# A perceiver megakernel: the second linear attention's query features get their 0.1 from ScalarE

## The chip, the cores and the metric

The kernel runs on one core of a Trainium2 chip. Its time is the device time of one execution in microseconds. Three runs were made; the figure used is their median. A separate execution was recorded by the hardware profiler, and all rows below come from it. The core has five engines with queues of their own: TensorE (PE in the rows, with PEld for its weight loads), VectorE (DVE), ScalarE (ACT), GpSimd (POOL) and SyncE (SP), which issues most transfers.

## The reference, cut to what matters

The program is a chain of eleven residual blocks over 16 sequences of 64 tokens, 256 wide (1024 tokens in all): three layers of cross attention, self attention and a feed-forward block, and a last layer that ends with its attention. The change lies in the eighth block, the self attention of the third layer, which the reference writes as

```python
def _spherical_features(x, projection):
    x_norm = x / (jnp.linalg.norm(x, axis=-1, keepdims=True) + 1e-08)
    proj = jnp.einsum('bhsd,hfd->bhsf', x_norm, projection)
    return jax.nn.relu(proj) + YAT_EPS          # YAT_EPS = 0.1
...
Qp = _spherical_features(Q, projection)
Kp = _spherical_features(K, projection)
KV = jnp.einsum('bhsf,bhsd->bhfd', Kp, V)
QKV = jnp.einsum('bhsf,bhfd->bhsd', Qp, KV)
K_sum = jnp.sum(Kp, axis=2)
normalizer = jnp.einsum('bhsf,bhf->bhs', Qp, K_sum)[..., None]
out = QKV / jnp.maximum(normalizer, 1e-06)
```

It has 16 heads of 16 channels, and 64 features for each head. Q, K and V are linear maps of the normalized input; the result goes through one more linear map and is added to the input. The query features `Qp` are the rectified projection plus 0.1.

## The kernel before

The eleven blocks are methods that issue their instructions one after the other; a tile framework places buffers, derives the waits from the data, and may order instructions within the engines' queues. Inside `l2_attn` (lines 1947 to 2118) `self.pinned` is on, so TensorE's instructions (issued by `mm`, line 2619, and `tr`, line 2631) keep the order in which the program writes them. `awake` issues matmuls whose result nobody reads.

`linear(i)` prepares one half of the tokens (512 of 1024) and is a generator, so that its steps can be laid between other work: it normalizes and transposes the input, and ScalarE copies the transposed blocks to `xT` (line 1989); `lin` multiplies by the weights for q, k and v; VectorE adds the biases (`z`, line 2007, and `va`, line 2003); ScalarE squares, VectorE sums and inverts the norms, GpSimd scales (`z`, line 2019); the scaled q and k are transposed to `qn` and `nT` (copies of line 127 on VectorE and 129 on ScalarE). Then come the query features: for each of two groups of channels, TensorE makes `pqp` in a PSUM tile of four banks (`quad`, one buffer, shared with the keys' `pkp`), ScalarE rectifies it into `qp` in SBUF (line 2040), and GpSimd adds 0.1 to the 128x2048 numbers in place (line 2041). So these two lines run twice in each half, four times in all.

The loop at line 2103 goes over eight blocks of 128 tokens and two steps more. Step t makes the keys' features of block t (`pkp` on TensorE, then `kp` on VectorE, line 2055, with maximum and 0.1 in one instruction), multiplies the queries of block t-1 with the sums of their sequences (`acc`, in `apply`, which reads `qp`), runs some steps of `linear(1)` while t is below 4, forms the sums of block t (`pk`, then four masked products `kv` on VectorE, lines 2070 and 2071), and projects block t-2 (`lin` with `wo`), adds it to `x` (line 425) and takes its mean and variance (`measured`, lines 145 and 146). For every second block `factors` turns the variance into a factor: a small multiply-add on VectorE (line 153), a root on ScalarE (line 154) and a reciprocal on VectorE (line 155). The query features of the second half come in step 3; they are read from step 5 on. Those of the first half come before step 0 and are read from step 1 on.

Of the kernel before, what the change touches and what calls it, by code (L numbers as in the profile page):

```python
# [12 lines left out]
F32 = mybir.dt.float32  # L13
I32 = mybir.dt.int32
BF16 = mybir.dt.bfloat16
AF = mybir.ActivationFunctionType
ALU = mybir.AluOpType
# [3 lines left out]
P = 128  # L21
# [43 lines left out]
class Sections:  # L65
# [1881 lines left out]
    def l2_attn(self):  # L1947
        nc, tc, d = self.nc, self.tc, self.d
        F, HT = 64, NT // 2
        with ExitStack() as ctx:  # L1950
            sb = ctx.enter_context(tc.tile_pool(name="l2a", bufs=1, side="right", reuse_waits="tile"))
# [15 lines left out]
            nc.gpsimd.memset(same, 0.0)  # L1967
            for h in range(2):
                nc.gpsimd.memset(same[h * S : (h + 1) * S, h * 16 : h * 16 + 16], 1.0)
            va = sb.tile([P, NT, 8, 33], F32, tag="va", name="va")  # L1970
            nc.gpsimd.memset(va[:, :, :, 32:33], 1.0)
            hT = sb.tile([P, KC, T], F32, tag="hT", name="hT")
            nT, qp = [None, None], [None, None]

            def quad(name):
                return ps.tile([P, 4, 512], F32, tag="quad", name=name)

            def linear(i):

                x = self.x[:, i * HT : (i + 1) * HT, :]  # L1980
                xln = sb.tile([P, HT, D], F32, tag=f"xln{i}", name="xln")
                xT = sb.tile([P, KC, 512], F32, tag=f"xT{i}", name="xT")
                for t in range(0, HT, 2):
                    pt = ps.tile([P, KC, 2, P], F32, tag="mm", name="tr", bufs=2)
                    for j in range(2):
                        self.normed(i * HT + t + j, xln[:, t + j, :])
                        for c in range(KC):
                            self.tr(pt[:, c, j, :], xln[:, t + j, c * P : (c + 1) * P], self.ident)
                    nc.scalar.copy(xT[:, :, t * P : (t + 2) * P], pt.rearrange("p c j x -> p c (j x)"))
                    yield  # L1990

                nc.gpsimd.tensor_tensor(x, x, bo.unsqueeze(1).to_broadcast([P, HT, D]), ALU.add)
                zs = []
                for t0 in range(0, HT, 2):
                    z = sb2.tile([P, 2, 2 * D], F32, tag="z", name="z")
                    for j in range(2):
                        t = t0 + j
                        for n, cols in ((2 * D, slice(0, 2 * D)), (D, slice(2 * D, 3 * D))):
                            pm = ps.tile([P, n], F32, tag="mm", name="lin", bufs=2, padded_shape=[P, 512])
                            for k in range(KC):  # L2000
                                self.mm(pm, xT[:, k, t * P : (t + 1) * P], w[:, k, cols], start=(k == 0), stop=(k == KC - 1))
                            if n == D:
                                nc.vector.tensor_tensor(
                                    va[:, i * HT + t, :, :32], pm.rearrange("p (a v) -> p a v", v=32),
                                    bv.rearrange("p (a v) -> p a v", v=32), ALU.add)
                            else:
                                nc.vector.tensor_tensor(z[:, j], pm, rows[:, : 2 * D], ALU.add)
                        if j == 0:
                            yield

                    sq = sb2.tile([P, 2, 2 * D], F32, tag="sq", name="sq")
                    nc.scalar.activation(sq, z, AF.Square)
                    ln = sb2.tile([P, 4 * H], F32, tag="ln", name="ln")
                    nc.vector.tensor_reduce(ln, sq.rearrange("p t (h e) -> p (t h) e", e=16), AX.X, ALU.add)
                    nc.scalar.activation(ln, ln, AF.Sqrt)
                    nc.vector.tensor_scalar(ln, ln, 1e-8, None, ALU.add)
                    nc.vector.reciprocal(ln, ln)
                    z4 = z.rearrange("p t (h e) -> p (t h) e", e=16)
                    nc.gpsimd.tensor_tensor(z4, z4, ln.unsqueeze(2).to_broadcast([P, 4 * H, 16]), ALU.mult)
                    zs.append(z)  # L2020
                    yield
                nT[i] = sb.tile([P, KC, 512], F32, tag=f"nT{i}", name="nT")
                qn = sb.tile([P, KC, 512], F32, tag=f"xT{i}", name="qn")
                for t0, z in zip((0, 2), zs):
                    self.awake(ps, 4 if i == 0 and t0 else 0, "mm", 2)
                    for dst, lo in ((qn, 0), (nT[i], D)):
                        pt = ps.tile([P, KC, 2, P], F32, tag="mm", name="tr", bufs=2)
                        for j in range(2):
                            for c in range(KC):
                                self.tr(pt[:, c, j, :], z[:, j, lo + c * P : lo + (c + 1) * P], self.ident)  # L2030
                        self.copy(dst[:, :, t0 * P : (t0 + 2) * P], pt.rearrange("p c j x -> p c (j x)"))
                    yield
                qp[i] = sb.tile([P, KC, 4, 512], F32, tag=f"qp{i}", name="qp")
                for g in range(KC):
                    self.awake(ps, 2 * g, "mm", 2)
                    pm = quad("pqp")
                    for r in range(4):
                        o = slice(32 * r, 32 * r + 32)
                        self.mm(pm[:, r, :], proj[o, g].rearrange("p h f -> p (h f)"), qn[o, g, :], start=True, stop=True)
                    nc.scalar.activation(qp[i][:, g], pm, AF.Relu)  # L2040
                    nc.gpsimd.tensor_scalar(qp[i][:, g], qp[i][:, g], 0.1, None, ALU.add)
                    yield

            def key_features(t):
# [54 lines left out]
            for _ in linear(0):  # L2099
                pass  # L2100
            rest = linear(1)
            kvs = {}
            for t in range(NT + 2):
# [896 lines left out]
```

## Time and profile before

| what | us |
|---|---|
| median of three runs (3728.47 to 3732.46) | 3731.08 |
| the profiled execution's own time | 3730.16 |
| its span, first to last instruction | 3728.4 |
| `l2_attn`, from its first `lin` on q, k, v to the last `lin` with `wo` | about 2981 to 3094 |
| line 2040, ScalarE's relu, four times | 1.877 each |
| line 2041, GpSimd's add, four times | 5.37 each |
| line 1932, a ScalarE pass SBUF to SBUF of the same size, in another block | 1.911 |

How to read the rows that follow. In a timeline a row gives the start in us of the span, the duration in us, the engine, the line of the kernel, the operation, the tiles it writes and reads, the shapes, how many such instructions the row joins, and in brackets how long the engine sat idle just before and who ended that wait. A row that joins several instructions may overlap the rows of the same engine a little. In a table by windows a row gives the stretch, its length, the busy time and the number of instructions of TensorE, its weight loads, VectorE, ScalarE and GpSimd, then the clock that TensorE was granted (1.00 is full speed), and the transfers' share. The chain that ended last is followed back from the last instruction, each step to what released it.

### The profile page before, as it was taken

To read this page: it belongs to the slowest core of one execution; us is meant where nothing else is said; L and a number is where in the kernel's file an instruction comes from. 1 tells how busy PE (TensorE), PEld (TensorE's weight loads), DVE (VectorE), ACT (ScalarE), POOL (GpSimd) and SP (SyncE) were. 2 spreads that over 40 slices of the span, in tenths; PEclk is the share of its full clock that TensorE was granted. 3 is DMA by queue.
4 is the path that set the end of the run, shared out by engine and by line. 5 is a ranking of instruction groups with operands and counts; after the bars stand their busy time and mean duration, and the time that the engine had idled before them with its cause. 6 is when DMAs were issued, how large, how long until landed. Compare 5 with 4: busy or idle time off the path is not lost.

```text
span 3728.4 us, 71203 instructions
## 1 busy us (share of the span) xinstructions
PE 3499.4 (94%) x31177; PEld 2200.2 (59%) x31192; DVE 1970.9 (53%) x3645; ACT 1461.2 (39%) x2093; POOL 1286.4 (35%) x784
## 2 busy tenths in 40 slices
PE   9999999998999979999988989999999889999997
PEld 4555555564665655555555666667767655555554
DVE  5344333436555635655656555577767765333445
ACT  2333333333444413444433443466666612111123
POOL 2555555552101113433422100577777630000002
PEclk9999999999999979999999999999999989999998
DMA  4111001101333345442101001211111004111550
GB/s 146 38 38 38 28 30 38 38 8 50 101 93 97 116 133 170 147 147 85 64 26 41 1 6 41 72 57 38 57 38 38 11 2 175 36 41 33 241 214 13
DMA packets 108071, 259.77 MB, mean 70 GB/s; under 512 B 9609, under 2 KB 76172, under 8 KB 105456
## 3 DMA queue, kind: packets, MB, share of 16 engines
q1 hardware_dynamic: 99040, 223.14, 16.8%
q10 hardware_dynamic: 6912, 27.27, 2.3%
q0 software_dynamic: 1808, 4.80, 0.5%
q8 instruction: 245, 4.01, 0.4%
q14 instruction: 66, 0.54, 0.0%
HBM read 248.85 MB, written 6.33 MB: 68 GB/s over the span
## 4 chain that ended last, share of the span: by engine, by line
PE 75%; DVE 13%; ACT 7%; issue 2%; DMA 1%; POOL 0%; SPq 0%; ACTq 0%; DVEq 0%; POOLq 0%
PE sc L2619 15%; PE pk L2619 15%; PE lin L2619 6%; PE acc L2619 6%; PE lin_t L2619 5%; ACT e L358 5%; PE pu L2619 4%; PE gate L2166 3%; PE up L2166 3%; PE lin L216 3%; PE pc L1786 3%; PE prz L2619 2%; PE gelu_t L1700 2%; PE turn L2631 1%; PE pa L2619 1%
## 5 line engine op out<-in xcount | busy, mean ns | idle before, releaser
L2548 POOL TENSOR_TENSOR tot<-tot,e 128x1024 f32<-128x1024 f32 (+1 forms) x340 | 803.2, 2362 | 373.3 <-ACT e L358 251.0
L299 DVE TENSOR_REDUCE m<-sc 128x4 f32<-128x2048 f32 x96 | 220.1, 2293 | 271.3 <-PE sc L2619 270.2
L1929 DVE SCALAR_TENSOR_TENSOR e<-sc,row_L_xattn_nbias,free 128x2048 f32<-128x2048 f32 x104 | 244.3, 2349 | 115.5 <-PE sc L2619 113.1
L1931 ACT ACTIVATE e<-e 128x2048 f32<-128x2048 f32 x104 | 198.7, 1911 | 245.8 <-DVE e L1929 245.8
L358 ACT ACTIVATE e<-sc 128x2048 f32<-128x2048 f32 x104 | 195.2, 1877 | 237.3 <-PE sc L2619 235.7
L2619 PE MATMUL sc<-qb,kT 32*128 32x128 f32 x6656 | 245.0, 283 | 36.2 <-DVE m L313 12.3
L2619 PEld LDWEIGHTS sc<-qb,kT 32*128 32x128 f32 x6656 | 206.1, 187 | 80.6 <-issue 22.4
L2619 PEld LDWEIGHTS acc<-e,v 128*32 128x32 f32 x6656 | 169.7, 109 | 105.3 <-issue 96.0
L2619 PE MATMUL acc<-e,v 128*32 128x128 f32 x6656 | 225.9, 276 | 4.7 <-ACT e L1932 4.7
L2619 PE MATMUL pk<-wv,cT 128*128 128x256 f32 x832 | 209.8, 394 | 0.0
L2619 PE MATMUL pk<-cT,wk 128*128 128x512 f32 (+1 forms) x512 | 206.2, 531 | 3.6 <-DVE rows L329 3.6
L1932 ACT ACTIVATE e<-e 128x2048 f32<-128x2048 f32 x104 | 198.7, 1911 | 3.2
L2619 PE MATMUL pk<-wkv,cT 128*128 128x256 f32 x832 | 196.3, 386 | 0.0
L2619 PE MATMUL pk<-cT,wkv 128*128 128x512 f32 (+1 forms) x512 | 194.9, 522 | 0.0
L2619 PEld LDWEIGHTS pk<-wv,cT 128*128 128x128 f32 x832 | 149.5, 190 | 76.4 <-issue 58.9
L2619 PEld LDWEIGHTS pk<-wkv,cT 128*128 128x128 f32 x832 | 153.2, 190 | 28.5 <-issue 4.3
L1786 PE MATMUL pc<-ew,eh 128*128 128x256 f32 x640 | 156.1, 386 | 0.0
L2170 ACT ACTIVATE g<-gate 128x512 f32<-128x512 f32 x68 | 40.6, 597 | 293.4 <-PE gate L2166 293.4
L2619 PE MATMUL sc<-kT,qb 32*128 32x512 f32 (+2 forms) x1536 | 138.9, 461 | 13.8 <-DVE m L299 2.3
L1319 POOL TENSOR_TENSOR e<-e,mx 128x512 f32<-128x512 f32 x96 | 81.9, 885 | 194.3 <-DVE mx L1318 194.3
L2619 PE MATMUL pu<-cn,e 128*64 128x257 f32 (+1 forms) x1248 | 141.6, 381 | 3.3 <-DMA cn<-in_ctx_n 1.8
L2171 DVE TENSOR_TENSOR hT<-up,g 128x512 f32<-128x512 f32 x68 | 47.0, 691 | 183.2 <-PE up L2166 183.2
(544 smaller groups left out, 6425.2 us busy)
## 6 DMA issues: line engine op xcount, KB each, us to landing
cT<-in_ctx_t SPq DMA_DIRECT2D x128, 832.0 KB, 6.4
cn<-in_ctx_n SPq DMA_DIRECT2D x32, 1664.0 KB, 11.9
piece<-in_ctx_n ACTq DMA_DIRECT2D x32, 640.0 KB, 3.9
w<-in_L_attn_W SPq DMA_DIRECT2D x8, 1024.0 KB, 7.0
piece<-in_ctx_n ACTq DMA_DIRECT2D x16, 384.0 KB, 3.7
w<-in_L_ffn_W SPq DMA_DIRECT2D x16, 256.0 KB, 3.1
down<-in_L_ffn_w_down SPq DMA_DIRECT2D x16, 256.0 KB, 2.8
gate<-in_L_ffn_w_gate SPq DMA_DIRECT2D x16, 256.0 KB, 2.7
```

What stands on the lines that cost most here:

```text
L216: nc.tensor.matmul(pm, xT[:, k, t * P : (t + 1) * P], w[:, k, :], start=(k == 0), stop=(k == kc - 1))
L299: nc.vector.tensor_reduce(x.m4[:, g, :, i], pm, AX.X, ALU.max)
L358: nc.scalar.activation(e, pm, AF.Exp, scale=0.25)
L1319: pin(nc.gpsimd.tensor_tensor(p.e, p.e, p.mx.unsqueeze(2).to_broadcast(p.shape), ALU.subtract))
L1700: nc.tensor.matmul(pm, w[:, c, lo : lo + m], cT[:, c, :], start=(c == 0), stop=(c == nk - 1))
L1786: nc.tensor.matmul(pc[:, n, j, :], s.eh[i][:, c, tok], ew2[:, c, cols], start=False, stop=(c == 3))
L1929: nc.vector.scalar_tensor_tensor(e16, pm16, nb, free[:, at : at + P].unsqueeze(1).to_broadcast([P, 16, P]), ALU.add, ALU.mult)
L1931: nc.scalar.activation(e, e, AF.Relu)
L1932: nc.scalar.activation(e, e, AF.Square)
L2166: nc.tensor.matmul(pm[-1], w[:, k, n * P : (n + 1) * P], xT[:, k, tok], start=(k == 0), stop=(k == KC - 1))
L2548: nc.gpsimd.tensor_tensor(tot[:w], x.first if c == 1 else tot[:w], e[:w], ALU.add)
L2619: ins = self.nc.tensor.matmul(*args, **kw)
```

## The change

GpSimd's add of 0.1 on the query features (line 2041) is replaced by a ScalarE pass on the same tile in place: identity with a bias that is read from a 128x1 tile `tenth`, which GpSimd fills with 0.1 once at the start of `l2_attn`. Relu and add remain two instructions, now on one engine.

```diff
             for h in range(2):
                 nc.gpsimd.memset(same[h * S : (h + 1) * S, h * 16 : h * 16 + 16], 1.0)
+            tenth = sb.tile([P, 1], F32, tag="tenth", name="tenth")
+            nc.gpsimd.memset(tenth, 0.1)
             va = sb.tile([P, NT, 8, 33], F32, tag="va", name="va")
...
                     nc.scalar.activation(qp[i][:, g], pm, AF.Relu)
-                    nc.gpsimd.tensor_scalar(qp[i][:, g], qp[i][:, g], 0.1, None, ALU.add)
+                    nc.scalar.activation(qp[i][:, g], qp[i][:, g], AF.Identity, bias=tenth)
                     yield
```

Every order on TensorE and VectorE stays as it was. ScalarE's order becomes relu, add, relu, add, where it was relu, relu; in the first half two copies of `xT` follow, in the second half the roots of line 154. The products `acc` wait for ScalarE's adds where they waited for GpSimd's.

## The prediction

> **What bounds the kernel now.** I read the page first, then the timeline of the second linear attention (2980 to 3090 us of the span), then the granted clock in slices.
>
> ```profile
> span 3728.4 us, 71203 instructions
> PE 3499.4 (94%) x31177; PEld 2200.2 (59%) x31192; DVE 1970.9 (53%) x3645; ACT 1461.2 (39%) x2093; POOL 1286.4 (35%) x784
> PE 75%; DVE 13%; ACT 7%; issue 2%; DMA 1%; POOL 0%; SPq 0%; ACTq 0%; DVEq 0%; POOLq 0%
> ```
>
> TensorE carries the whole kernel. GpSimd has 0% of the chain that ended last, so shortening its work pays only where something else waits for it. The edited line runs four times. The timeline of its first half:
>
> ```profile
> 3004.54 1.88 ACT L2040 ACTIVATE qp<-pqp 128x2048 f32<-128x2048 f32 x1 [0.93 <-PE pqp L2619]
> ...
> 3006.50 10.83 POOL L2041 TENSOR_SCALAR qp<-qp 128x2048 f32<-128x2048 f32 x2 [4.67 <-ACT qp L2040]
> 3007.54 1.98 PE L2619 MATMUL awake<-cst 128*128 128x512 f32 x4
> 3007.68 1.88 ACT L2040 ACTIVATE qp<-pqp 128x2048 f32<-128x2048 f32 x1 [1.26 <-PE pqp L2619]
> ...
> 3009.61 0.73 PE L2619 MATMUL pkp<-proj,nT 32*128 32x128 f32 x16
> 3010.26 1.09 PE L2631 MATMUL tr<-cst,xln 128*128 128x128 f32 x8
> ...
> 3010.96 1.07 ACT L1989 COPY xT<-tr 128x512 f32<-128x512 f32 x2 [1.40 <-PE tr L2631]
> 3011.59 2.85 PE L2619 MATMUL lin<-wqkv,xT 128*128 128x512 f32 x8 [0.24 <-ACT xT L1989]
> ```
>
> Here nobody waits for GpSimd: its second add ends at 3017.33, and the products of `qp` continue at 3017.53 behind a mask product of VectorE that ended at 3017.48. But ScalarE stands on the path: the second relu (to 3009.56) frees the PSUM tile for `pkp`, and its copy of `xT` releases `lin`. The second half:
>
> ```profile
> 3051.49 10.81 POOL L2041 TENSOR_SCALAR qp<-qp 128x2048 f32<-128x2048 f32 x2 [17.55 <-ACT qp L2040]
> 3052.53 1.86 PEld L2619 LDWEIGHTS pk<-va,kp 64*128 64x128 f32 x32 [0.76 <-issue]
> 3052.53 1.98 PE L2619 MATMUL pk<-va,kp 64*128 64x33 f32 x32
> 3052.66 1.88 ACT L2040 ACTIVATE qp<-pqp 128x2048 f32<-128x2048 f32 x1 [1.26 <-PE pqp L2619]
> ...
> 3057.01 5.31 DVE L153 TENSOR_SCALAR xr<-xm 128x2 f32<-128x2 f32 x1
> 3060.51 1.82 DVE L2055 TENSOR_SCALAR kp<-pkp 128x1024 f32<-128x1024 f32 x1
> ...
> 3062.40 3.62 PE L2619 MATMUL pk<-va,kp 64*128 64x33 f32 x32 [5.15 <-DVE kp L2055]
> ```
>
> Line 153 works on 128x2 numbers; its median over 21 runs is 164 ns, and here it takes 5.31 us. GpSimd's fourth add starts at 3056.9 and, at 5.37 us, ends at 3062.3; line 153 ends at 3062.32. I take this as VectorE locked out while GpSimd holds something that they share. A second instance supports it: the 128x256 line 158 takes 2.30 us from 2980.45 (median 0.405) and ends, within 0.15 us, with GpSimd's line 1992 (2980.25 to 2982.60). `kp` is queued behind line 153 on VectorE, TensorE waits 5.15 us for `kp`, and afterwards runs at half clock:
>
> ```profile
> 3057.20:3062.30 5.10, 0.05 (x4) 0.00 (x0) 5.10 (x2) 0.00 (x0) 5.10 (x1) 1.00 0.00 0
> 3062.30:3069.10 6.80, 6.70 (x52) 5.61 (x52) 4.44 (x11) 0.20 (x1) 0.12 (x2) 0.50 0.00 0
> ```
>
> The figure after the five engines is TensorE's granted clock: 1.00 while it idles, 0.50 for the 6.8 us that follow.
>
> **Removed: four GpSimd adds, 4 x 5.37 = 21.5 us.** As busy time worth nothing: the first products that read each half's `qp` come after the adds' ends anyway. GpSimd's next work is `z` at 3026.17, after 8.84 us idle, and a memset at 3062.36 whose tile is needed a stage later. What counts is the lockout. Without it line 153 ends near 3057.15, `kp` runs 3057.1 to 3058.3 (1.21, its usual time) instead of ending at 3062.33. **Gain A: 4.0 us**, and TensorE's idle shrinks from 5.15 to about 1.1 us. What is late next is `kp` itself behind its matmuls, as in every later iteration.
>
> **Gain B, the clock after it.** Low, `pk` took 3.62, `lin` 2.07 and `pkp` 1.24 us; in the next iterations they take 1.98, 1.13 and 0.73. At full clock VectorE is the limit: from one `kp`'s end to the next one's start takes 4.3 us (3070.48 to 3074.78); here it took 6.93 (3062.33 to 3069.26). So B is between 0 (the clock falls anyway) and 2.6 us. The Trainium skill, page "TensorE: Matmul & The Clock Gate", section "Part 1: The HAM clock gate", says that TensorE's clock goes to half after at least one idle window of some 3.4 us. By that rule 1.1 us of idling leaves the clock up and B is 2.6. The trace disagrees: at 3031.5 the clock went to 0.50 when the 3.5 us before it (3028.0 to 3031.5) were 3.09 us busy with `pk`, `pkp` and a few `acc`, short matmuls like those around 3058. In the three iterations from 3069 to 3084, with idles of 0.3 to 0.8 us, it stayed at 1.00. My 1.1 us lies between these rows, so I take half: **B = 1.3 us**, both ends kept for the range.
>
> **Added: four ScalarE passes, 128x2048, SBUF to SBUF, with a bias from memory.** No row has this exact form. Without a bias operand the same shape takes 1911 ns (line 1932, 104 times). An operand from memory adds 687 - 597 = 90 ns at 128x512 (lines 2711 and 2170) and 1115 - 1057 = 58 at 128x1024. So 1.97 to 2.00 us each; I take 1.98. The skill's page "ScalarE: Activation LUTs", section "What ACT_TABLE_LOAD costs", gives about 1.99 us at this size for a bias that is a pointer operand. Two adds lie on the path below: with the page's figure the sum would be 0.02 us higher, with the plain row 0.14 lower.
>
> First half, with starts chained (0.03 us between dependent passes, as from line 1931 to 1932; 0.1 us overlap between independent ones, as in the pair of `xT` copies): relu to 3006.42, add to 3008.43, second relu 3008.33 to 3010.21 instead of 3009.56, so `pkp` starts 0.65 later; second add 3010.24 to 3012.22; `xT` copy from 3012.12 instead of 3010.96. `lin` starts 1.16 us later. Everything to the second half hangs from `lin` through TensorE's pinned order, `z`, the squares and the transposes, and I see no slack there that isn't itself behind `lin`. **Cost C: 1.2 us** (0.65 if part of it is absorbed, 1.4 with longer passes). Queued behind the adds on ScalarE are only that relu, the two `xT` copies, and a square that waits 9.67 us anyway.
>
> Second half: the second relu goes from 3052.66 to about 3053.3 and ends at 3055.2; `pkp` needs its tile at 3055.49. Cover 0.3 us; gone, it would cost what exceeds it. The last add runs to 3057.2 on an idle ScalarE; the next entry, the small root of line 154, needs line 153 (3057.15) in any case. The readers of `qp` come at 3062 or later. Cost 0.
>
> **Small things at nothing.** The new memset (0.1 us, like its neighbours at 2959.7) sits in a GpSimd queue that then idles 20.09 us. No extra table load appears in ScalarE's list (121 both ways). Two instructions much later wait for ScalarE's adds instead of GpSimd's, both long done: one context transfer on SP's queue near 3096 (weights and other contexts behind it) and one GpSimd subtraction. No DMA is moved.
>
> **Sum.** -4.0 - 1.3 + 1.2 = -4.1 us. The profiled execution took 3730.16 us (3728.4 of span and 1.8 around it), 0.9 under the median of 3731.08. 3730.16 - 4.1 = 3726.1 for that execution; against the median, 3731.08 - 4.1 = 3727.0.
>
> **Rivals.**
> *The clock stays up* (20%). B is 2.6: -4.0 - 2.6 + 1.2 = -5.4, 3725.7. For it: the page's rule and the three later iterations. Against: 3031.5.
>
> *The clock falls in the first half* (14%), the case that ends slower. From 3009.5, where the `awake` matmuls end, to 3012.75 TensorE would have only `pkp` and transposes, 3.2 us instead of 2.1. If the clock falls there, `lin` x8 and what follows run slow. Priced by rows at 0.50 (`pk` +1.6, `pkp` +0.5, `acc` +0.8, each four 512-wide matmuls +1.5, so `lin` x8 with its narrower half about +2.3 and the next four +1.5): +6.7 if it stays low to 3021, about half for two 3.4 us stretches. It turns the result once its price passes A + B - C = 4.1, so when the clock stays low for some 8 us (half of each is lost); with the whole 6.7 it gives 3731.08 + 6.7 - 4.1 = 3733.7. For it: the fall at 3031.5. Against: the dense `lin` and `awake` around the gap, and a similar gap of 2.0 us at 3001.3 to 3003.3, transposes only, left the clock at 1.00.
>
> *The lockout isn't GpSimd's doing* (6%): line 153 stalls for another reason, and C alone remains: 3732.3. Against: ends that agree within 0.02 us, and the second instance.
>
> The forecast itself has 60%, its own range 3724 to 3730.
>
> **How the numbers follow.** 0.2% of the time is 7.5 us, about what a measurement of this kernel can tell from no change. Faster by over that needs B whole and luck with the clock elsewhere (the three runs of before spread 4 us): 0.13, from the first rival and the edge of the forecast. Slower by over that needs the second rival at its worst and B lost: 0.05. The rest, 0.82, is within. The range takes in the first rival (3725.7) with the runs' spread of some 4 us below it and the third (3732.3) and second (3733.7) above: 3721.5 to 3734.0.
>
> **What would show it.** Line 153 at about 0.16 us in all of its places in this stage, `kp` at 1.2; `lin` after the first `xT` copy about 1.2 us later against the first relu; four new passes near 1.98 us; the second half's `pkp` not waiting for the relu; a clock row at about 3060 that says whether B came. It is wrong if line 153 stays long, if the clock falls near 3012, or if the stage's gain is taken back before the next stage begins.

## The result, and the profile after

The changed kernel takes 3721.25 us (median of 8 runs, 3717.72 to 3725.91), the kernel before in the same session 3730.9 us (8 runs). The ratio is 0.9977 with a 95% interval of 0.9967 to 0.9986: some 8.6 us faster (5.2 to 12.3). Against the median of the first table that is 0.9977 x 3731.08 = 3722.5 us. The forecast was 3727.0, a gain of 4.1: the direction and the place were right, the size was about half. The 3722.5 us lie below the forecast's own 3724 to 3730 and 1 us inside the outer range of 3721.5 to 3734.0.

The profiled execution of the changed kernel took 3725.91 us, the slowest of its eight. Its page, busy time by engine and then the chain that ended last:

```profile
span 3724.1 us, 71203 instructions
...
PE 3496.8 (94%) x31177; PEld 2199.2 (59%) x31192; DVE 1966.5 (53%) x3645; ACT 1468.6 (39%) x2097; POOL 1264.3 (34%) x781
...
PE 75%; DVE 13%; ACT 7%; issue 2%; DMA 1%; POOL 0%; SPq 0%; ACTq 0%; DVEq 0%; POOLq 0%
```

ScalarE has four instructions more (2097 for 2093), GpSimd three fewer (four adds less, one memset more), and the shares of the chain are those of before. Nothing on this page tells where the time went. In the timeline of the first half the line numbers are higher by two than before:

```profile
3009.74 1.88 ACT L2042 ACTIVATE qp<-pqp 128x2048 f32<-128x2048 f32 x1 [0.93 <-PE pqp L2621]
...
3011.71 2.00 ACT L2043 ACTIVATE qp<-qp,tenth 128x2048 f32<-128x2048 f32 x1
...
3013.62 1.86 ACT L2042 ACTIVATE qp<-pqp 128x2048 f32<-128x2048 f32 x1
...
3015.51 2.00 ACT L2043 ACTIVATE qp<-qp,tenth 128x2048 f32<-128x2048 f32 x1
...
3015.53 0.73 PE L2621 MATMUL pkp<-proj,nT 32*128 32x128 f32 x16 [0.80 <-ACT qp L2042]
...
3017.42 1.05 ACT L1991 COPY xT<-tr 128x512 f32<-128x512 f32 x2
...
3018.04 2.85 PE L2621 MATMUL lin<-wqkv,xT 128*128 128x512 f32 x8 [0.76 <-ACT xT L1991]
```

ScalarE now runs from 3009.74 to 3018.5 without a pause, and `lin` waits for it: 8.30 us after the first relu (3018.04 - 3009.74), where it was 7.05 (3011.59 - 3004.54). That is the cost C. The second half, from the last relu on:

```profile
3054.30 1.86 ACT L2042 ACTIVATE qp<-pqp 128x2048 f32<-128x2048 f32 x1
...
3056.19 2.00 ACT L2043 ACTIVATE qp<-qp,tenth 128x2048 f32<-128x2048 f32 x1
...
3056.45 0.73 PE L2621 MATMUL pkp<-proj,nT 32*128 32x128 f32 x16
...
3057.97 0.17 DVE L153 TENSOR_SCALAR xr<-xm 128x2 f32<-128x2 f32 x1
3058.05 1.22 DVE L2057 TENSOR_SCALAR kp<-pkp 128x1024 f32<-128x1024 f32 x1
...
3059.32 2.33 PE L2621 MATMUL pk<-va,kp 64*128 64x33 f32 x32 [1.11 <-DVE kp L2057]
...
3061.57 2.07 PE L2621 MATMUL lin<-wo,hT 128*128 128x256 f32 x4
...
3064.88 1.22 DVE L2057 TENSOR_SCALAR kp<-pkp 128x1024 f32<-128x1024 f32 x1 [0.77 <-PE pkp L2621]
```

Line 153 takes 0.17 us instead of 5.31, TensorE waits 1.11 us for `kp` instead of 5.15. But `pk` with 2.33 us is partly, and `lin` with 2.07 wholly, at half clock. The table by windows says when the clock fell, in the columns named ahead of the prediction: first relu to third relu, third relu to the end of `kp`, the stretch after the fall, and the last 75 VectorE instructions of the program (its last attention):

```profile
3009.74:3050.48 40.74, 34.02 (x437) 21.58 (x438) 24.82 (x43) 12.40 (x12) 3.87 (x2) 1.00 0.01 2
3050.48:3059.27 8.79, 7.64 (x128) 4.87 (x128) 4.94 (x13) 7.83 (x5) 0.12 (x1) 1.00 0.01 2
3060.78:3074.43 13.65, 13.65 (x190) 11.24 (x192) 9.74 (x19) 0.00 (x0) 0.00 (x0) 0.50 0.01 2
3673.20:3724.10 50.90, 33.87 (x678) 21.38 (x678) 31.24 (x75) 22.81 (x46) 10.24 (x14) 0.89 0.07 22
```

The first and the last of these stretches in the kernel before:

```profile
3004.54:3049.53 44.99, 40.47 (x437) 27.09 (x438) 25.26 (x43) 8.63 (x11) 14.62 (x4) 0.81 0.01 2
3674.70:3728.40 53.70, 37.09 (x678) 22.54 (x678) 31.23 (x75) 22.56 (x46) 10.08 (x13) 0.84 0.07 21
```

Both stretches hold the same TensorE work in both kernels (437 and 678 matmul records), yet TensorE is busy for 6.5 and 3.2 us longer in before, because its granted clock was lower (0.81 for 1.00, 0.84 for 0.89). So one pair of traces splits as follows, after less before, in us: up to the first relu +5.2 (identical instructions), first to third relu -4.25, third relu to the end of `kp` -4.01, from there to the end of the stage's last `lin` with `wo` +0.2, rest of the program -1.4; together -4.3. Only the third term is a wait of the instructions alone. The others mix in where the clock happened to fall, and a single pair cannot separate them.

### The profile page after: what moved, and what is told of

It is laid out like the page before. It is cut to its first block, busy times and chain, and to the rows that moved or that the text cites. A ratio compares the mean times of both kernels' runs of the same rounds, so it can differ in the third digit from the quotient of the medians.

```text
span 3724.1 us, 71203 instructions
## 1 busy us (share of the span) xinstructions
PE 3496.8 (94%) x31177; PEld 2199.2 (59%) x31192; DVE 1966.5 (53%) x3645; ACT 1468.6 (39%) x2097; POOL 1264.3 (34%) x781
## 3 DMA queue, kind: packets, MB, share of 16 engines
q8 instruction: 245, 4.01, 0.4%
## 4 chain that ended last, share of the span: by engine, by line
PE 75%; DVE 13%; ACT 7%; issue 2%; DMA 1%; POOL 0%; SPq 0%; ACTq 0%; DVEq 0%; POOLq 0%
PE pk L2621 15%; PE sc L2621 15%; PE lin L2621 6%; PE acc L2621 6%; PE lin_t L2621 5%; ACT e L358 5%; PE pu L2621 4%; PE gate L2168 3%; PE up L2168 3%; PE lin L216 3%; PE pc L1786 3%; PE prz L2621 2%; PE gelu_t L1700 2%; PE turn L2633 1%; PE pa L2621 1%
## 5 line engine op out<-in xcount | busy, mean ns | idle before, releaser
L2621 PE MATMUL sc<-kT,qb 32*128 32x512 f32 (+2 forms) x1536 | 138.5, 460 | 13.8 <-DVE m L299 2.3
```

What stands on the lines that cost most here:

```text
L2621: ins = self.nc.tensor.matmul(*args, **kw)
```

## What had to be told apart

The theory: GpSimd's add locks VectorE out of line 153 (A); lifting that gains 4.0 us and something through the clock (B); ScalarE's two adds in the first half cost 1.2 (C). The rivals: the second half has nothing to do with it, and the time changed in the first half; the gain comes from less work on GpSimd or from the clock alone; line 153 is long for another reason. Open besides: why the gain is twice the sum.

Every ratio below is against the kernel before on the same chip, with its 95% interval; differences in us are (ratio - 1) x 3730. The ratio is estimated from all runs, so it can differ by 1 to 2 us from the quotient of two medians. Line numbers shift with every edit; the tiles tell which instruction a row is.

## Experiments: which half, and which instruction

**Only the second half by ScalarE.**

```diff
-                    nc.scalar.activation(qp[i][:, g], qp[i][:, g], AF.Identity, bias=tenth)
+                    if i == 1:
+                        nc.scalar.activation(qp[i][:, g], qp[i][:, g], AF.Identity, bias=tenth)
+                    else:
+                        nc.gpsimd.tensor_scalar(qp[i][:, g], qp[i][:, g], 0.1, None, ALU.add)
```

> ScalarE adds the 0.1 in the second half only; the first half keeps GpSimd's add, so the delay of 1.2 us there is gone and the lockout of line 153 is still lifted. If the gain of the change lies in the lockout (4.0 us, plus 1 to 3 us of clock behind it), this kernel is faster than before by 5 to 7 us, and at least 1 us faster than the whole change; line 153 is short. If the gain of the change (8.6 us) came mostly from the first half, from the clock staying up between 3031 and 3048 because ScalarE's passes shift the work, then this kernel keeps the low stretch there and gains only 4 us or less.

Measured: 3719.89 us (9 runs), ratio 0.9977 (0.9967 to 0.9987), -8.6 us. Its timeline in the second half:

```profile
3054.70 0.17 DVE L153 TENSOR_SCALAR xr<-xm 128x2 f32<-128x2 f32 x1
3054.78 1.22 DVE L2060 TENSOR_SCALAR kp<-pkp 128x1024 f32<-128x1024 f32 x1
...
3056.05 1.98 PE L2624 MATMUL pk<-va,kp 64*128 64x33 f32 x32 [1.11 <-DVE kp L2060]
```

The whole gain is there with half of the change: the second half is enough for it. The rival, that the gain came from the clock in the first half, does not fit, since this trace still spends 13.7 us at half clock between the first and the third relu (17.1 in before). Nor is it 1 us faster than the whole change, as I had expected with the cost C gone; the intervals cannot tell.

**Only the first half by ScalarE**: the same edit with `i == 0`.

> ScalarE adds the 0.1 in the first half only; the second half keeps GpSimd's add, so line 153 is locked out for about 5.3 us as before. By the lockout theory this kernel is slower than before by the ScalarE cost alone, 1.2 us (0.5 to 2). By the theory that the first half brought the gain through the clock, it is faster by 4 us or more, with the clock at 1.00 through the transposes of the second half's z.

Measured: 3727.94 us (13 runs), ratio 0.9997 (0.9989 to 1.0006), -1.1 us. The lockout is back:

```profile
3053.77 10.82 POOL L2046 TENSOR_SCALAR qp<-qp 128x2048 f32<-128x2048 f32 x2 [12.11 <-ACT qp L2042]
...
3059.29 5.33 DVE L153 TENSOR_SCALAR xr<-xm 128x2 f32<-128x2 f32 x1
3062.80 1.82 DVE L2060 TENSOR_SCALAR kp<-pkp 128x1024 f32<-128x1024 f32 x1
...
3064.70 3.62 PE L2624 MATMUL pk<-va,kp 64*128 64x33 f32 x32 [5.17 <-DVE kp L2060]
```

GpSimd's two adds end at 3064.59, line 153 at 3064.62, as before within 0.03 us. Half of GpSimd's work is gone and no gain is clear of the noise (interval -4.1 to +2.2): its busy time is not what counts. The cost C, which the timeline shows, is not to be seen in the time either.

**The victim moved, the adds left where they were.** All four adds stay on GpSimd. Within this stage ScalarE takes line 153's addition into its root as a bias (`eps` is a 128x1 tile of 1e-5).

```diff
-        nc.vector.tensor_scalar(r, self.xm[:, lo:hi, 1], 1.0, 1e-5, ALU.mult, ALU.add)
-        nc.scalar.activation(r, r, AF.Sqrt)
+        if self.eps is not None:
+            nc.scalar.activation(r, self.xm[:, lo:hi, 1], AF.Sqrt, bias=self.eps)
+        else:
+            nc.vector.tensor_scalar(r, self.xm[:, lo:hi, 1], 1.0, 1e-5, ALU.mult, ALU.add)
+            nc.scalar.activation(r, r, AF.Sqrt)
```

> The adds stay on GpSimd; within this block the factor's multiply-add on VectorE (line 153) is dropped, and ScalarE takes the root of variance plus 1e-5 with the 1e-5 as a bias from memory. If GpSimd's add locks VectorE out only for that instruction, nothing stalls: kp of block 4 ends 4 us earlier, the time falls by 5 to 7 us, without any change to the adds. If something else stalls VectorE there, the stall moves to the next instruction (kp shows some 5 us) and the time stays within 1 us of before.

Measured: 3721.02 us (12 runs), ratio 0.9981 (0.9973 to 0.999), -7.1 us.

```profile
3048.77 10.81 POOL L2048 TENSOR_SCALAR qp<-qp 128x2048 f32<-128x2048 f32 x2 [16.73 <-ACT qp L2047]
...
3054.18 1.19 DVE L2062 TENSOR_SCALAR kp<-pkp 128x1024 f32<-128x1024 f32 x1
3054.30 0.30 ACT L156 ACTIVATE xr<-xm,eps 128x2 f32<-128x2 f32 x1 [2.47 <-DVE xm L146]
3055.28 0.16 DVE L160 RECIPROCAL xr<-xr 128x2 f32<-128x2 f32 x1
...
3055.43 1.98 PE L2626 MATMUL pk<-va,kp 64*128 64x33 f32 x32 [0.89 <-DVE kp L2062]
3055.79 1.75 DVE L2094 RECIPROCAL rec<-rec 128x256 f32<-128x256 f32 x1
```

This separates the wait from the work. GpSimd works as long as before, to 3059.6, and the gain comes all the same, because the one instruction that it locked out is no longer VectorE's. The row of `kp` shows more: it reads PSUM, and it ran at its usual 1.19 us beneath GpSimd's add. Nor does every VectorE instruction that works from SBUF to SBUF wait: the two reciprocals in the rows took their usual 0.16 and 1.75 us beneath the same add. What sets line 153 apart from them no run here shows.

**Relu and add in one VectorE instruction** (maximum with 0, plus 0.1, from PSUM; neither ScalarE nor GpSimd takes part).

```diff
-                    nc.scalar.activation(qp[i][:, g], pm, AF.Relu)
-                    nc.gpsimd.tensor_scalar(qp[i][:, g], qp[i][:, g], 0.1, None, ALU.add)
+                    nc.vector.tensor_scalar(qp[i][:, g], pm, 0.0, 0.1, ALU.max, ALU.add)
```

> Relu and 0.1 in one VectorE instruction from PSUM (maximum, then add), no pass on ScalarE or GpSimd. By the row of kp (1.21 us for 1024) it takes about 2.3 us each. The lockout is gone (4.0 us and 1 to 3 us of clock). In the first half each of the two steps takes 0.4 us longer than the relu did: 0.8 us. In the second half VectorE is busy with a reciprocal when the first one is ready, so it starts 1.3 us late and the pinned matmuls behind it shift by some 2 us. Sum: 2 to 4 us faster than before, less than second_only. If VectorE has room there after all, 5 to 7 us faster.

Measured: 3720.78 us (11 runs), ratio 0.9976 (0.9967 to 0.9985), -9.0 us, not to be told from the changed kernel. That is more than expected (2 to 4 us, or 5 to 7 with room on VectorE). One such pass takes longer than ScalarE's relu, but there is no second one:

```profile
3009.29 2.29 DVE L2040 TENSOR_SCALAR qp<-pqp 128x2048 f32<-128x2048 f32 x1 [1.26 <-PE pqp L2618]
```

The delays came as expected: the first `pkp` 0.83 us later against the first pass, and the third pass 1.2 us late behind a reciprocal on VectorE. What the expectation missed is the clock: this trace spends 3.4 us at half clock from the first pass to the end of the last `lin` with `wo`, where before spends 27.3.

## Experiments: the wait put back, and the clock

**A wait of about the lockout's size on VectorE in the changed kernel**: a reciprocal that nobody reads, queued ahead of `kp` of block 4.

```diff
+                    if t == 4:
+                        nc.vector.reciprocal(idle, self.xm[:, 1, 1:2].to_broadcast([P, 750]))
```

> The changed kernel with a VectorE reciprocal of 128x750 numbers (a result that nobody reads; about 5.1 us by 1.75 us for 256) put between line 153 and kp of block 4, so that kp is as late as under the lockout, with GpSimd idle. If the whole gain of the change is the wait of TensorE for that kp with what follows from it, this kernel is back at before plus the first half's delay: -1 to +2 us against before, and the clock falls behind it. If part of the gain comes from GpSimd's absence elsewhere, it keeps that part: 2 us or more under before.

Measured: 3727.35 us (13 runs), ratio 0.9996 (0.9988 to 1.0004), -1.5 us: the gain is gone, though all four adds are ScalarE's.

```profile
3054.13 0.17 DVE L153 TENSOR_SCALAR xr<-xm 128x2 f32<-128x2 f32 x1
3054.20 4.83 DVE L2110 RECIPROCAL idle<-xm 128x750 f32<-128x750 f32 x1
3058.98 1.20 DVE L2058 TENSOR_SCALAR kp<-pkp 128x1024 f32<-128x1024 f32 x1
...
3060.24 3.63 PE L2624 MATMUL pk<-va,kp 64*128 64x33 f32 x32 [5.87 <-DVE kp L2058]
```

The wait came out 0.7 us longer than the lockout's (5.87 for 5.15 on TensorE), so it takes back a little more than A.

**The clock alone, first try.** The kernel before with eleven products in block 4 that nobody reads, between `pkp` and `pk`, to keep TensorE busy through the lockout.

```diff
+                for _ in range(11 if t == 4 else 0):
+                    self.mm(pk[:, 0, :], self.ident, self.cst[:, :512], start=True, stop=True)
```

> The kernel before, with 11 matmuls of 512 columns (0.43 us each, 4.7 us) that nobody reads, put into TensorE's wait for kp in block 4, so that TensorE is busy during the lockout. The lockout stays: line 153 takes 5.3 us and kp ends as late as before. If the clock that falls behind the lockout is worth 2 to 4 us, this kernel is faster than before by that much and the clock stays at 1.00 after block 4's pk. If the clock behind it is worth nothing, it is within 1 us of before.

Measured: 3729.88 us (13 runs), ratio 0.9999 (0.9991 to 1.0007), -0.4 us. The experiment was mis-sized. I had taken one product as one pass of 0.43 us; it is two:

```profile
3053.05 9.71 PE L2621 MATMUL pk<-cst 128*128 128x512 f32 x22
```

The filling went on 4.5 us after `kp` had ended, and the time was still no longer. In the trace the clock held until 3070.0 and then fell for 3.4 us only. So the clock may have given back about what the overrun cost, which is a hint of its price and no measurement of it.

**The clock alone, second try**: five products.

> The kernel before with TensorE kept busy through the lockout, now with 5 filler products of two passes each (10 x 0.43 = 4.3 us, inside the wait of 5.15), so that kp's end isn't overrun as it was with 11. If the fall of the clock behind the lockout is worth what the timelines of the kernels without lockout say, the time falls by 2 to 4 us with line 153 still at 5.3 us; if that fall costs nothing, it stays within 1 us of before.

Measured: 3728.42 us (13 runs), ratio 0.9993 (0.9985 to 1.0002), -2.6 us (-5.6 to 0.7).

```profile
3065.96 5.31 DVE L153 TENSOR_SCALAR xr<-xm 128x2 f32<-128x2 f32 x1
3066.13 4.56 PE L2621 MATMUL pk<-cst 128*128 128x512 f32 x10
3069.45 1.82 DVE L2055 TENSOR_SCALAR kp<-pkp 128x1024 f32<-128x1024 f32 x1
...
3071.35 1.98 PE L2621 MATMUL pk<-va,kp 64*128 64x33 f32 x32 [0.66 <-DVE kp L2055]
...
3076.52 1.19 DVE L2055 TENSOR_SCALAR kp<-pkp 128x1024 f32<-128x1024 f32 x1
```

```profile
3071.30:3078.13 6.83, 5.30 (x123) 4.43 (x124) 6.42 (x14) 0.20 (x1) 0.12 (x1) 1.00 0.01 2
3078.13:3084.95 6.82, 6.82 (x79) 5.70 (x80) 4.48 (x8) 0.00 (x0) 0.00 (x0) 0.50 0.01 2
```

The lockout is the same, TensorE fills it, and `pk` after it runs at full clock (1.98 us, not 3.62). From this `kp`'s end to the next one's start it now takes 5.25 us (3071.27 to 3076.52) instead of 6.93, so 1.7 us come back at this place. But the clock fell one block later, at 3078.13, for the same 6.8 us: the filling put the fall off and did not take it away. From the third relu to the end of the last `lin` with `wo` this trace takes 43.16 us, before 44.23. The 2.6 us of the timed runs, whose interval includes zero, are therefore no price of one fall.

**The changed kernel, filled in its shorter waits**: two products in block 4, one in each of blocks 5 to 7, with the edit above inside the changed kernel.

> The changed kernel with 2 such matmuls in TensorE's wait for kp in block 4 (1.1 us) and 1 in each of blocks 5 to 7, where TensorE waits 0.3 to 0.8 us. If short waits with little matmul work let the clock fall there in some executions, the time is 1 to 3 us under the changed kernel and the clock holds at 1.00 from block 4 to block 7. If the clock isn't decided there, it is within 1 us of the changed kernel, or up to 0.5 us slower.

Measured: 3716.72 us, but only 5 runs, ratio 0.9963 (0.995 to 0.9977), -13.8 us. Measured again:

> The changed kernel with fillers in blocks 4 to 7 again, since the first interval rests on five runs only (13.8 us under before). By the timelines the fillers save up to 3 us where the clock would have fallen: 8 to 11 us under before. If the five runs were a chance draw, it equals the changed kernel at about 8.

Measured: 3719.19 us (8 runs), ratio 0.9973 (0.9963 to 0.9984), -10.1 us. And the same filling in the kernel whose second half alone is ScalarE's:

> ScalarE's add in the second half only, GpSimd's in the first, and the fillers of the kernel above: no delay in the first half, no lockout, no fall of the clock in blocks 4 to 7. If all three are worth what the timelines say, it is the fastest: 8 to 10 us under before, 1 to 3 us under the changed kernel. If the first half's delay and the fillers are worth nothing, it equals the changed kernel within 1 us.

Measured: 3722.8 us (16 runs), ratio 0.998 (0.9972 to 0.9987), -7.5 us. The three intervals overlap with that of the changed kernel. Filling may help by a few us or not at all; it is not a version that beats it by these runs.

**Two controls.** The changed kernel and the kernel before, each measured once more.

> The changed kernel itself once more, for a second trace and a second interval. From the timelines, the change takes 4.0 us out of the stretch from the third relu to the end of block 4's kp in every execution, and some 3 us of clock behind it; the first half costs 1.2 us. That gives 5 to 7 us faster. If the first measurement (8.6 us) holds, something else brings 2 to 3 us; if the clock in the first half is decided by where its windows fall, the stretch from the first to the third relu differs between two traces of this one kernel by 3 to 5 us.

> The kernel before itself, as one more of the compared kernels: its ratio to before must include 1, and how far it strays tells what 0.1% means here. Its trace shows once more line 153 at 5.3 us and a fall of the clock behind it that lasts two or three stretches of 3.4 us; the stretch from the first to the third relu and the last attention block show whether falls elsewhere repeat from one execution to the next.

Measured: the changed kernel 3722.11 us (12 runs), ratio 0.9978 (0.997 to 0.9987), -8.2 us; the kernel before against itself 3729.94 us (13 runs), ratio 0.9999 (0.9991 to 1.0007). The gain repeats, and the comparison shows none where there is none. In the second trace of the changed kernel the clock fell at another place: for 10.25 us in the first half, while behind the lifted wait it stayed up.

```profile
3003.06:3047.52 44.46, 38.63 (x437) 25.37 (x438) 25.12 (x43) 12.40 (x12) 3.87 (x2) 0.88 0.01 2
3036.41:3046.66 10.25, 10.25 (x124) 8.51 (x128) 4.78 (x11) 0.59 (x1) 0.00 (x0) 0.50 0.01 2
```

```profile
3055.09 1.22 DVE L2057 TENSOR_SCALAR kp<-pkp 128x1024 f32<-128x1024 f32 x1
...
3056.36 1.98 PE L2621 MATMUL pk<-va,kp 64*128 64x33 f32 x32 [1.11 <-DVE kp L2057]
...
3060.38 1.21 DVE L2057 TENSOR_SCALAR kp<-pkp 128x1024 f32<-128x1024 f32 x1
```

First to third relu took 44.46 us here and 40.74 in the other trace of the same kernel; from `kp` of block 4 to the next `kp` 4.07 us here (3060.38 - 3056.31) and 5.61 there (3064.88 - 3059.27). So the stretch behind the wait in a single trace cannot give the size of B. Only the third relu to the end of `kp` is the same in every trace: 12.80 us in both of before, 8.79 in both of after, 8.56 to 8.79 in each of the other kernels without a lockout or a wait in its place (in the VectorE kernel from the third pass).

## The clock over all runs

Every timed run lists its span and its mean granted clock, and in these traces the clock is either 1.00 or about 0.50. So the time at half clock of a run is 2 x (1 - clock) x span. One listing is coarse (a step of 0.001 is 7.5 us), but the runs can be averaged. The kernel before spent 158.5 us at half clock (105 runs, standard error 0.65), the changed kernel 142.5 (20 runs, standard error 1.6): 16 us less, where the prediction had counted on 6.8 at most. Among the 105 runs of before, whose instructions are all the same, the time rises by 0.42 us (standard error 0.03) for each us at half clock. That gives two terms for every kernel: what its trace shows on the path of the instructions (A, C, the overrun or the longer wait told above), and 0.42 times the change of its time at half clock against before on the same chip.

| kernel | path, us | half clock, us | 0.42 x | sum | measured |
|---|---|---|---|---|---|
| second half only | -4.0 | -13.2 | -5.5 | -9.5 | -8.6 |
| first half only | +1.25 | -5.6 | -2.4 | -1.1 | -1.1 |
| root by ScalarE | -4.2 | -7.6 | -3.2 | -7.4 | -7.1 |
| changed, again | -4.0 + 1.25 | -17.6 | -7.4 | -10.1 | -8.2 |
| changed, with the wait put back | +0.75 + 1.25 | -8.1 | -3.4 | -1.4 | -1.5 |
| before, eleven products | +4.5 | -13.9 | -5.8 | -1.3 | -0.4 |
| before, five products | 0 | -5.8 | -2.4 | -2.4 | -2.6 |
| before, again | 0 | -1.2 | -0.5 | -0.5 | -0.4 |

Each sum lies within 2 us of its time. The one-instruction VectorE kernel and the filled ones are left out, since I did not work out their path in full; at half clock the first is 16.3 us below before, and the filled ones 28.7, 26.0 and 14.4. With the path of the kernels that they were made from (-2.75, -2.75 and -4.0) the filled ones would come to -14.8, -13.7 and -10.1, against -13.8, -10.1 and -7.5 measured: up to 3.6 us off. The slope is an association among runs, no intervention, and a standard error of 2 to 4 us stands on each kernel's half-clock time, so the table supports the account and does not prove its second decimal.

Two traces of each kernel show where most of it vanished. The stage from the first relu to the end of the last `lin` with `wo`, first in the two traces of before, then in the two of the changed kernel:

```profile
3004.54:3093.76 89.22, 75.47 (x1024) 52.85 (x1024) 59.33 (x107) 12.99 (x15) 25.46 (x7) 0.85 0.01 2
3007.59:3096.86 89.27, 75.53 (x1024) 52.92 (x1024) 59.31 (x107) 12.99 (x15) 25.45 (x7) 0.85 0.01 2
...
3009.74:3090.86 81.12, 70.31 (x1024) 49.23 (x1024) 55.27 (x107) 20.64 (x19) 3.98 (x3) 0.92 0.01 2
3003.06:3084.05 80.99, 70.41 (x1024) 49.01 (x1024) 54.86 (x107) 20.64 (x19) 3.98 (x3) 0.92 0.01 2
```

The stage is 8.1 to 8.3 us shorter, about the whole measured gain, and the two traces of a kernel agree, wherever the clock fell. Of it, -4.0 + 1.25 are the path. The remaining 5.4 us go with the clock: the same 1024 matmuls keep TensorE busy for 5.1 us less, and the stage spends 13.7 us at half clock instead of 27.3. The fall behind the lockout is only 6.8 of these; the largest, 17.1 us, lies between the first and the third relu in both traces of before. There all seven traces with GpSimd's adds in the first half have 10 to 17 us at half clock, and the six with ScalarE's have none (four) or 10 (two). That is a count over traces. Why the clock fell less often there, where ScalarE's adds delay the work by 1.25 us, is not shown.

Outside the stage less is clear. The last attention of the program, some 600 us later, spent 53.70 x 0.16 x 2 = 17 us at half clock in before and 50.90 x 0.11 x 2 = 11 in after. From the end of the last `lin` with `wo` to the end of the program the five traces with the lockout by GpSimd took 634.6 to 636.4 us, the nine without it 631.6 to 634.7, for the same instructions. Why a change so far ahead should decide it is not settled, and one kernel without the lockout (the changed one, filled) had a last attention as long as before's. In these traces the low stretches last 3.4, 6.8, 10.25, 13.65 and 17.1 us, so they come in steps of some 3.41; no experiment moved these steps by themselves.

## Why the prediction was right, and where it was off

- **A, the lockout (forecast -4.0).** Right in cause, place and size. From the third relu to the end of `kp`: 12.80 to 8.79 us, -4.01. That GpSimd's add is the cause was argued from two ends that agree; it is now shown from four sides: the gain goes with the half that has the add, it goes when the add comes back, it comes when the victim alone is moved, and it goes when another wait takes the lockout's place. The rival that line 153 stalls for another reason falls.
- **What is late next.** `kp` behind its matmuls, with TensorE waiting 1.11 us; forecast about 1.1.
- **C, the first half (forecast +1.2).** 1.25 us in the timeline, with `pkp` 0.72 later (forecast 0.65) and the adds at 2.00 us (1.98). So the one form that no row had shown was well bounded by its neighbours, and the 1.99 us of the Trainium skill's page "ScalarE: Activation LUTs", section "What ACT_TABLE_LOAD costs", agrees too. In the times C does not show: first half only was 1.1 us faster than before, not 1.2 slower (interval -4.1 to +2.2). In its trace the stretch from the first to the third relu had no time at half clock (17.1 us in before), which more than paid for it there.
- **The second half's cover (0.3 us).** The last relu ended at 3056.16 and `pkp` began at 3056.45: 0.29 us, and `pkp` waited for nobody. GpSimd's shortened work was worth nothing, as forecast.
- **B, the clock (forecast -1.3).** This is the term that was mis-sized. I had priced one fall at 0 to 2.6 us and taken half. In the stage as a whole the clock was worth 5.4 us in both pairs of traces; over all runs the change lowers the time at half clock by 16 us, which at 0.42 is 6.7. With -4.0 and +1.25 the two give -8.2 and -9.5, against -8.6 and -8.2 measured. The error was to look for the clock's answer only in the 7 us behind the wait, when the larger part of it lay elsewhere in the stage. No run took the fall behind the wait away by itself, so its own price stays open.
- **The rule that was weighed.** By the section "Part 1: The HAM clock gate" of the Trainium skill's page "TensorE: Matmul & The Clock Gate", the clock falls after an idle window of some 3.4 us. In the first trace of after it fell at 3060.78, although TensorE had been busy for 7.64 of the 8.79 us up to 3059.27 and had not waited longer than 1.11 (in the last 3.41 us before the fall it was busy for 2.30, with `acc` and `pk`, at most 64 wide); in the second trace of the same kernel it held at the same place and fell at 3036.41, behind 3.41 us with nothing but transposes (1.76 us busy). So the trace of before, with its fall at 3031.5 after a busy stretch, was the better guide, as I took it. But neither told me that the fall would come in some executions and not in others.
- **The range, and luck.** A gain above 7.5 us was given a chance of 0.13 and was to need B whole "and luck with the clock elsewhere". That outcome came, and twice (8.6 and 8.2 us), so it was no lucky draw; it was a term left out. The lowest outcome that the prediction had priced was 3725.7. That its outer range took in 3722.5 is due to the 4 us allowed below that for the spread of the runs, which in this sense was luck.
- **The rivals.** "The clock stays up" (3725.7) was nearer than the forecast, for one of two traces as told and still too small. "The clock falls in the first half near 3012" did not occur in any of the six traces that have ScalarE's adds there.

## What to carry to other kernels

An engine with 0% of the chain that ended last can still set the time: look for a tiny instruction whose longest case is many times its median and which ends together with a long one of another engine. The cure can be on either side: moving the long work away and moving the one small victim gained the same here within the noise (8.2 to 8.6 and 7.1 us). And where TensorE's clock may fall, a removed wait can be worth more or less than its length. So compare TensorE's busy time for the same matmuls over the whole stage, in more than one trace, and average the granted clock over many runs, before explaining the last few us from the place next to the wait.

## What the runs showed of the hardware

- A VectorE multiply-add on 128x2 numbers in SBUF took 5.31 us instead of 0.16 beneath a GpSimd add on 128x2048 and ended with it, while a VectorE instruction of 128x1024 that reads PSUM (1.19 us) and VectorE reciprocals from SBUF to SBUF (0.16 and 1.75 us) ran at their usual speed beneath the same kind of add.
- The clock fell behind 3.41 us of narrow matmuls (2.30 us busy) in one execution of the changed kernel, behind 3.41 us of transposes (1.76 busy) in the other, and the first one came through the same transposes (3040.30 to 3043.71, 1.93 busy) at 1.00. The two executions differ by 3.7 us from the first to the third relu, over the same 437 matmuls.
- A product of 128x512 in f32 with a weight of 128x128 counts as two matmuls of 0.44 to 0.46 us each (22 in 9.71 us, 10 in 4.56).
